# Attention's product with W as seven block products, and an order of work that is planned five times

## The chip, the cores and the metric

The kernel runs on one core of one Trainium2 chip. The metric is device time in microseconds (us) of one execution. The core has these engines: PE (TensorE, matrix products; its weight loads, PEld, run beside them), DVE (VectorE), ACT (ScalarE), POOL (GpSimd) and SP, which here only issues DMAs.

## The reference, cut to what matters

```python
# x: 128 graphs x 128 nodes x 256, float32; adj: 128 x 128 x 128, about 1/8 ones
h = relu(layernorm(x))
for i in range(3):                                   # a gated graph network, OUT = 256
    aggr = einsum('bst,bsd->btd', A, h @ weight[i])
    h = gru_cell(aggr, h, w_ih, w_hh, b_ih, b_hh)
x = x + h
h = relu(layernorm(x))                               # graph attention
Wh = h @ W                                           # W: 256 x 256
s = Wh.sum(-1)
e = where(adj == 0, -inf, leaky_relu(s[:, :, None] + s[:, None, :], 0.2))
x = x + softmax(e) @ Wh
```

The kernel computes the last line as (softmax(e) @ h) @ W: first the weighted sums of h, then their product with W. That product is what changes.

## The kernel before, in words

**Groups and phases.** The 128 graphs are worked on in 32 groups of 4 (G = 4, NG = 32). Each group passes three layers of the graph network and then attention. The 96 pairs (group, layer) are put one after another in `turns` (line 919), so that three groups at different layers are in flight; each pair has a slot of SLOT = 18150 ns.

**A planner orders everything.** Nothing is issued when the Python code meets it. Each piece of work is recorded with `op(engine, ns, function, reads, writes, ...)` (line 75): an engine, an assumed duration, and the buffers it touches. At the end `Plan.run` (line 122) counts due times back through the dependences (`rank_all`), and then places the operations one by one in an imagined course of the five engines, always the one that can begin first, by due time among equals. The order it finds is the order in which each engine gets its instructions; real semaphores hold the dependences. Once built, the order on each engine is fixed.

**The chain.** The products of the graph network (`product`, L719, 128x256 results; `product_rows`, L733, 128x384) form a chain whose order is given beforehand. Each gate product is a block scheme with seven products in place of eight; its data-side sums are made by `node_sums` (L688, L690, L692: on POOL for the state, on DVE for the neighbour sums). `DATA`, `unit` and `source` (lines 696 to 705) say which block or sum each of the seven products takes.

**Between the chain's products** PE gets the side work: `edge_sums` (L645: 12 short bf16 matmuls to a bank, the neighbour sums as exact three-part products), `weighted` (L674: attention's weighted sums, four 128x128 matmuls to each of two banks) and `rows_product` (L1110: the product with W). All of these use two PSUM banks, tag "misc", which the planner gives out as they come free.

**rows_product**, lines 1104 to 1121: for each pair of graphs it takes one misc bank, and for each graph and each half k of the 256 inputs multiplies a 128x128 block of uT (the transposed weighted sums, the stationary operand) by 256 columns of W. DVE then scales each graph's 256 columns by 1/denominator (rden) and adds them to x1 (L1119). A group has 8 such matmuls and 4 such additions. `inner` and late groups do the same in smaller steps.

**The beginning.** `weights()` (line 404) loads and transposes the weights; `compose` (L474) multiplies weight[i] with w_ih once for each layer, and `block_sums` forms the sums of weight blocks, for layer 0 on DVE and for the others and w_hh on POOL. In the first EARLY = 3 groups PE transposes the normed rows (`rows_to_T`, L555); later groups do it with two ACT copies, two DMA transposes and two ACT copies (`turned_halves`, L581, L591, L585).

**In the profile** every fp32 matmul has two records, since PE passes its data twice, and so has its weight load; a transpose of fp32 and a bf16 matmul have one.

Of the kernel before, what the change touches and what calls it, by code (L numbers as in the profile page):

```python
# [13 lines left out]
OP = mybir.AluOpType  # L14
AX = mybir.AxisListType

P = 128
G = 4
# [4 lines left out]
EARLY = 3  # L23
# [3 lines left out]
MARGIN = 7000  # L27
TIMED = 4
KB = 3
# [12 lines left out]
class Plan:  # L42
# [13 lines left out]
    def __init__(self, tags):  # L56
        self.tags = tags
        self.nodes, self.last, self.group, self.due, self.chain = [], {}, 0, 0, []
        self.marks, self.turns, self.waiting, self.phase = {}, [], {}, 0
# [15 lines left out]
    def op(self, eng, ns, fn, reads=(), writes=(), room=(), due=None, mark=None,  # L75
# [5 lines left out]
        i, deps = len(self.nodes), set()  # L81
        for b in room:
            if b.prev is not None:
                deps.update(a[0] for a in b.prev.accesses)
# [37 lines left out]
    def run(self):  # L122
        nodes = self.nodes
        users = [[] for _ in nodes]
        for i, n in enumerate(nodes):
            for j in n[3]:
                users[j].append(i)
        chain = sorted(self.chain, key=lambda i: nodes[i][5], reverse=True)
        bound = set(chain)
        waiting = {t: [b for _, _, b in sorted(w, key=lambda x: x[:2], reverse=True)]  # L130
                   for t, w in self.waiting.items()}

        after = [list(u) for u in users]
        for tag, w in waiting.items():
# [23 lines left out]
        rank_all()  # L158
        missing = [len(n[3]) for n in nodes]
        behind = [(i, self.marks[mark]) for i, mark in self.turns if mark in self.marks]  # L160
        for i, j in behind:
            nodes[i][5] = rank[j] + nodes[i][1]
            users[j].append(i)
            missing[i] += 1
        rank_all()
        for i, _ in behind:
            rank[i] = -float("inf")
        ready = {e: [] for e in self.LAG}
        at = [0.0] * len(nodes)
# [3 lines left out]
        clock, port, thin = dict.fromkeys(self.LAG, 0.0), 0.0, False  # L173
        slots = {t: [0.0] * n for t, (n, kind) in self.tags.items()
                 if kind in ("free", "turn")}
        order, end = [], 0.0
        while len(order) < len(nodes):
            best = None
            for e, pool in ready.items():
# [3 lines left out]
                for i in pool:  # L183
                    if i in bound and i != chain[-1]:
                        continue
                    t = max(clock[e] + (self.FLIP if thin and e == "PE" and not nodes[i][8] else 0), at[i])
                    for b in nodes[i][4]:
                        if b.slot is None:
                            t = max(t, min(slots[b.tag]))
# [13 lines left out]
            n = nodes[i]  # L203
            done = t + self.ns(i, t)
            clock[e] = done - self.OVER[e]
# [5 lines left out]
            for b in n[4]:  # L211
                if b.slot is None:
                    if b.tag in waiting:
                        waiting[b.tag].pop()
# [1011 lines left out]
```

## Time and profile before

| what | value |
|---|---|
| median of 3 runs (lowest, highest) | 2085.99 us (2085.65, 2086.52) |
| the profiled execution's own time | 2085.63 us |
| its span, first to last instruction | 2083.8 us |
| mean granted TensorE clock | 1.000 |
| PE busy, share of the span | 2075.7 us, 100% |
| DVE busy | 1661.7 us, 80% |
| ACT busy | 1599.6 us, 77% |
| POOL busy | 934.4 us, 45% |
| mean DMA rate | 66 GB/s |

The span lies 1.8 us below the execution's own time. A PE record's end is modelled and lies after the point where the next matmul may start, so records overlap: what a matmul takes from PE is read from the start of one to the start of the next, not from its length.

### The profile page before, as it was taken

What the parts mean: (1) busy time and instruction counts of PE and PEld (TensorE: products, weight loads), DVE (VectorE), ACT (ScalarE), POOL (GpSimd) and SP (SyncE); (2) the same over time, 40 slices, a digit from 0 to 9 for tenths busy, and PEclk for the clock granted to TensorE, in tenths of its full rate; (3) what the DMA queues carried; (4) which work ended last, traced back from release to release, by engine and by line L of the source; (5) the groups of instructions that cost most, each with busy time, mean ns of one, the idle gap of its engine ahead of it and who ended that gap; (6) DMA issues with size and microseconds to landing.
All of it is one profiled execution on the core that took longest, in us unless ns stands there. A gap on an engine that the chain in (4) does not pass through costs nothing.

```text
span 2083.8 us, 30778 instructions
## 1 busy us (share of the span) xinstructions
PE 2075.7 (100%) x10630; PEld 1662.7 (80%) x10630; DVE 1661.7 (80%) x3626; ACT 1599.6 (77%) x2977; POOL 934.4 (45%) x881
## 2 busy tenths in 40 slices
PE   9999999999999999999999999999999999999999
PEld 7887887777887778887778877788777788788776
DVE  7678888788788788788788778788778877878778
ACT  6577887877778687868778868778868777877686
POOL 6445554434454445444454344355344544445330
PEclk9999999999999999999999999999999999999999
DMA  3322323322223233232323232233232223223321
GB/s 117 76 61 46 56 49 74 73 56 60 66 72 66 61 72 66 54 83 61 73 56 81 47 86 61 63 70 81 46 81 61 60 56 78 49 54 66 72 77 40
DMA packets 365148, 137.02 MB, mean 66 GB/s; under 512 B 296384, under 2 KB 364736, under 8 KB 364992
## 3 DMA queue, kind: packets, MB, share of 16 engines
q1 hardware_dynamic: 364992, 135.05, 29.6%
q8 instruction: 84, 1.38, 0.3%
q14 instruction: 72, 0.59, 0.1%
HBM read 45.36 MB, written 16.78 MB: 30 GB/s over the span
## 4 chain that ended last, share of the span: by engine, by line
PE 99%; DMA 0%; DVE 0%; SPq 0%; ACT 0%; issue 0%; DVEq 0%; ACTq 0%
PE y_rz L719 16%; PE q_rz L719 11%; PE x_rz L719 11%; PE y_n L719 8%; PE misc L645 6%; PE y_n L733 6%; PE y_rz L733 6%; PE x_n L719 5%; PE q_n L719 5%; PE misc L1110 5%; PE q_n L733 4%; PE x_n L733 4%; PE q_rz L733 4%; PE x_rz L733 4%; PE misc L674 3%; PE misc L474 1%
## 5 line engine op out<-in xcount | busy, mean ns | idle before, releaser
L602 POOL TENSOR_TENSOR r<-rows 128x512 f32<-128x512 f32 x126 | 150.9, 1217 | 318.5 <-ACT rows L585 171.6
L775 DVE TENSOR_TENSOR t_rz<-t_rz,q_rz 128x512 f32<-128x512 f32 x192 | 131.4, 684 | 127.6 <-ACT t_rz L765 99.6
L688 POOL TENSOR_TENSOR hs<-hT 128x512 f32<-128x512 f32 x96 | 129.3, 1347 | 194.7 <-PE y_n L733 82.0
L765 ACT COPY t_rz<-y_rz 128x512 f32<-128x512 f32 x192 | 112.1, 584 | 125.5 <-PE y_rz L719 78.3
L719 PE MATMUL y_rz<-hs,s_hh 128*128 128x256 f32 x768 | 198.9, 382 | 0.0
L719 PE MATMUL y_rz<-gs,s_x 128*128 128x256 f32 x768 | 197.2, 379 | 0.0
L719 PEld LDWEIGHTS y_rz<-hs,s_hh 128*128 128x128 f32 x768 | 144.1, 190 | 22.9 <-ACT t_rz L765 4.7
L719 PEld LDWEIGHTS y_rz<-gs,s_x 128*128 128x128 f32 x768 | 146.2, 190 | 19.5
L775 DVE TENSOR_TENSOR t_n<-t_n,q_n 128x512 f32<-128x512 f32 x192 | 131.0, 682 | 32.5 <-ACT t_n L765 18.9
L605 POOL TENSOR_TENSOR p<-r 128x512 bf16<-128x512 f32 x126 | 153.3, 1234 | 0.2
L692 POOL TENSOR_TENSOR hs<-hT,hs 128x256 f32<-128x256 f32 x96 | 73.1, 761 | 171.2 <-PE q_n L733 118.8
L909 POOL TENSOR_TENSOR x<-x,u 128x512 f32<-128x512 f32 x60 | 80.9, 1364 | 134.4 <-DMA x<-in_x_dram 96.5
L719 PE MATMUL x_rz<-hT,s_hh 128*128 128x256 f32 x512 | 131.4, 379 | 0.0
L719 PE MATMUL x_rz<-aT,s_x 128*128 128x256 f32 x512 | 131.4, 379 | 0.0
L648 ACT COPY aT<-misc 128x512 f32<-128x512 f32 x190 | 105.9, 584 | 22.2 <-PE misc L645 20.4
L622 POOL TENSOR_TENSOR d<-hT,pl 128x512 f32<-128x512 f32 x64 | 80.3, 1256 | 87.1 <-ACT pl L620 40.7
L719 PE MATMUL y_n<-hs,s_hh 128*128 128x256 f32 x384 | 114.4, 380 | 0.0
L719 PE MATMUL y_n<-gs,s_x 128*128 128x256 f32 x384 | 114.3, 380 | 0.0
L1110 PE MATMUL misc<-w,uT 128*128 128x256 f32 x480 | 112.8, 379 | 0.0
L719 PEld LDWEIGHTS x_rz<-hT,s_hh 128*128 128x128 f32 x512 | 97.4, 190 | 19.2
L688 DVE TENSOR_TENSOR gs<-aT 128x512 f32<-128x512 f32 x96 | 78.6, 819 | 37.6 <-ACT aT L648 37.2
L719 PEld LDWEIGHTS x_rz<-aT,s_x 128*128 128x128 f32 x512 | 97.4, 190 | 13.0
(286 smaller groups left out, 6286.7 us busy)
## 6 DMA issues: line engine op xcount, KB each, us to landing
rows<-in_x_dram SPq DMA_DIRECT2D x32, 512.0 KB, 4.1
x<-in_x_dram SPq DMA_DIRECT2D x32, 512.0 KB, 3.9
out_dram<-x SPq DMA_DIRECT2D x31, 512.0 KB, 3.1
at<-in_adj_dram SPq DMA_DIRECT2D x32, 256.0 KB, 2.9
plT<-pl SPq DMA_TRANSPOSE x186, 3.3
peT<-pe SPq DMA_TRANSPOSE x60, 3.1
e<-in_L_gnn_weight_dram SPq DMA_DIRECT2D x3, 256.0 KB, 5.2
rz<-in_L_gnn_w_ih_dram SPq DMA_DIRECT2D x2, 384.0 KB, 4.3
```

The lines of the kernel that those rows point to most:

```text
L602: op("POOL", 1042, lambda part=part: nc.gpsimd.tensor_tensor(ap(r1)[:, part], ap(rows)[:, part], top(rows)[:, part], OP.subtract), [(rows, ...
L605: op("POOL", 1042, lambda part=part: nc.gpsimd.tensor_tensor(ap(p3)[:, part], ap(r1)[:, part], top(r1)[:, part], OP.subtract), [(r1, n, n ...
L622: op("POOL", 1158, lambda k=k, r=r: nc.gpsimd.tensor_tensor(ap(r), ap(hT)[:, k], part(pl, k, 0), OP.subtract), [(hT, 2 * k, 2 * k + 2), (p ...
L645: nc.tensor.matmul(flat(ps)[:, b * N:(b + 1) * N], part(i, b, k), ap(a)[:, b, :], start=(i == 0), stop=(i == 2))
L648: op("ACT", 590, lambda k=k, ps=ps: nc.scalar.copy(ap(dst)[:, k, :], flat(ps)), [ps], [(dst, 2 * k, 2 * k + 2)])
L688: op(eng, cost, lambda: sub(ap(w)[:, 0:2, :], blocks()[:, 1::2, :], blocks()[:, 0:2, :], OP.subtract), [t], [(w, 0, 2)], two=True)
L719: nc.tensor.matmul(ap(bank)[:, half, :], ap(w)[:, i - 1, gate, :], source(i, t, sums), start=(first and c == 0 and m == 0), stop=False, sk ...
L733: op("PE", 645, lambda c=c, w=w, t=t, sums=sums: nc.tensor.matmul(flat(bank)[:, c * P:(c + 3) * P], source(i, t, sums)[:, m * N:(m + 1) * ...
L765: op("ACT", 590, lambda: nc.scalar.copy(ap(t), ap(y)), [y], [t], mark=mark)
L775: op("DVE", 690, lambda: nc.vector.tensor_tensor(ap(t), ap(t), ap(q), OP.add), [q], [t])
L909: op("POOL", 1273, lambda cols=cols, part=part: nc.gpsimd.tensor_tensor(part(x1), part(x1), ap(u)[:, cols], OP.add), [(u, 2 * lo, 2 * hi)] ...
L1110: nc.tensor.matmul(ap(ps)[:, b, :], ap(uT)[:, k, (m + b) * N:(m + b + 1) * N], ap(w1)[:, k, :], start=(k == 0), stop=(k == KD - 1))
```

## The change

1. **Seven block products** (`seven_products`) take the place of `rows_product` in groups 0 to 25 (`g < NG - 6`). For each pair of graphs the transposed sums are seen as 2 x 2 blocks, and so is W. Seven products, each of one block or sum of blocks of uT with one block or sum of blocks of W, take the place of the eight. Each product is two matmuls of 128x128 (one for each graph of a pair). Four sums of blocks of W are made once, on POOL, in the tile w1, which grows to 8 blocks. The data-side sums are made in each group by DVE, into h1, when the weighted sums have been taken from it. The results gather in three half banks X, Q and Y; both misc banks are held. Product 1 goes into X, ACT copies X to Y, and products 2, 7, 6, 5, 3 and 4 add to X, Q and Y, while DVE takes partial results from Y between its products: 12 additions of 128x128 in place of 4 of 128x256.
2. **PSUM's written marks.** Edge sums and whole weighted sums now start a bank once, not each region, so that the whole bank counts as written (`set_bits`); other users of the bank unset the mark. Where the second bank isn't marked when product 1 begins, a matmul with zeros is put in.
3. **The plan.** `run` now places everything PASSES = 5 times (`place`) and keeps the plan whose imagined end is earliest. After each pass `latest` counts new due times back from that plan, with the buffers as it gave them out and with PE's idle time after START taken out; the operations of groups 27 and later (LAST) keep their first due times, moved as a whole. A misc buffer's users get urgent due times as soon as it is given out.
4. **The beginning.** EARLY goes from 3 to 1: groups 1 and 2 are now transposed by DMA. The load of w_hh is recorded with a longer time to landing (5000 in place of 3300 ns).

```diff
-EARLY = 3
+EARLY = 1
+URGENT = 10 ** 9
+PASSES, START, LAST = 5, 20000, 27
...
+        given = list(rank)
+        for _ in range(PASSES):
+            order, end, why, begun, clock, slot = self.place(users, list(rank), bound)
+            if best is None or end < best[0]:
+                best = end, order, clock, slot, begun, why
+            rank = self.latest(users, begun, slot, bound, given)
...
+                    if b.tag == "misc":
+                        for u in b.users:
+                            rank[u] = min(rank[u], t - URGENT)
...
-        "w1": (1, "all", const, [P, KD, D]), "w1_out": (1, "all", const, [P, KD]),
+        "w1": (1, "all", const, [P, 8, P]), "w1_out": (1, "all", const, [P, KD]),
...
-        load(w_hh_nat, nat, w_hh.rearrange("(c p) e -> p c e", p=P), 768)
+        load(w_hh_nat, nat, w_hh.rearrange("(c p) e -> p c e", p=P), 768, lag=5000)
...
+        for i, j, k, f in ((4, 1, 3, OP.add), (5, 4, 0, OP.subtract), (6, 0, 1, OP.subtract), (7, 2, 5, OP.subtract)):
+            op("POOL", 400, lambda i=i, j=j, k=k, f=f: nc.gpsimd.tensor_tensor(
+                ap(W["w1"])[:, i], ap(W["w1"])[:, j], ap(W["w1"])[:, k], f),
+               [(W["w1"], j, j + 1), (W["w1"], k, k + 1)], [(W["w1"], i, i + 1)])
...
-                                         ap(a)[:, b, :], start=(i == 0), stop=(i == 2))
+                                         ap(a)[:, b, :], start=(b == 0 and i == 0), stop=(i == 2),
+                                         skip_group_check=True)
+                set_bits(ps)
...
-        for m in range(lo, hi, 2):
+        if g < NG - 6:
+            seven_products(h1, uT, x1, rden)
+        for m in range(lo, hi, 2) if g >= NG - 6 else ():
...
+    def seven_products(sums, uT, x1, rden):
+        op("DVE", 690, lambda: nc.vector.tensor_tensor(
+            ap(sums)[:, 0:2, :], blocks_of(uT)[:, 1::2, :], blocks_of(uT)[:, 0:2, :], OP.subtract),
+           [uT], [(sums, 0, 2)], two=True)
+        op("DVE", 426, lambda: nc.vector.tensor_tensor(
+            ap(sums)[:, 2, :], ap(sums)[:, 1, :], blocks_of(uT)[:, 0, :], OP.add),
+           [uT, (sums, 1, 2)], [(sums, 2, 3)], two=True)
+        op("DVE", 426, lambda: nc.vector.tensor_tensor(
+            ap(sums)[:, 3, :], blocks_of(uT)[:, 2, :], ap(sums)[:, 2, :], OP.subtract),
+           [uT, (sums, 2, 3)], [(sums, 3, 4)], two=True)
+        one, two = buf("misc"), buf("misc")
+        X, Q, Y = (one, 0), (one, 1), (two, 0)
+        COLUMN = [None, 0, 2, 7, 3, 4, 5, 6]
+
+        def multiply(bank, i, first=False, room=()):
+            (b, h), c = bank, COLUMN[i]
+
+            def mm():
+                if first and written.get(two.slot) is None:
+                    nc.tensor.matmul(flat(two), zeros[:, :P], zeros, start=True, stop=True,
+                                     skip_group_check=True)
+                for m in range(2):
+                    nc.tensor.matmul(ap(b)[:, h, m * P:(m + 1) * P], source(i, uT, sums)[:, m * N:(m + 1) * N],
+                                     ap(W["w1"])[:, c], start=(first and m == 0), stop=True,
+                                     skip_group_check=True)
+                if first:
+                    set_bits(one)
+                    set_bits(two)
+            op("PE", 444, mm, [unit(i, uT, sums), (W["w1"], c, c + 1)], [(b, h, h + 1)], room)
+
+        def add(bank, j, n):
+            b, h = bank
+            for m in range(2):
+                i = 2 * n + m
+                op("DVE", 286, lambda i=i, m=m: nc.vector.scalar_tensor_tensor(
+                    ap(x1)[:, i, j * P:(j + 1) * P], ap(b)[:, h, m * P:(m + 1) * P], ap(rden)[:, i:i + 1],
+                    ap(x1)[:, i, j * P:(j + 1) * P], op0=OP.mult, op1=OP.add),
+                   [(b, h, h + 1), rden], [(x1, i, i + 1)])
+
+        multiply(X, 1, True, [two])
+        op("ACT", 390, lambda: nc.scalar.copy(ap(two)[:, 0], ap(one)[:, 0]), [(one, 0, 1)], [(two, 0, 1)])
+        multiply(X, 2)
+        add(X, 0, 0)
+        multiply(Q, 7)
+        multiply(Y, 6)
+        add(Y, 1, 0)
+        multiply(Y, 5)
+        add(Y, 1, 1)
+        add(Q, 1, 1)
+        multiply(Y, 3)
+        add(Y, 0, 1)
+        multiply(Q, 4)
+        add(Q, 1, 0)
```

## The prediction

> **What bounds the kernel now.** I read the page's busy times first, then the chain that ended last, then PE's own waits, and then the timeline of one stretch in the middle, for what a matmul takes from PE.
>
> ```profile
> PE 2075.7 (100%) x10630; PEld 1662.7 (80%) x10630; DVE 1661.7 (80%) x3626; ACT 1599.6 (77%) x2977; POOL 934.4 (45%) x881
> PE 99%; DMA 0%; DVE 0%; SPq 0%; ACT 0%; issue 0%; DVEq 0%; ACTq 0%
> ```
>
> PE is busy for the whole span, and the chain runs along PE alone: no other engine releases anything late. PE's waits by line:
>
> ```profile
> PE misc L374 <- DMA rz<-in_L_gnn_w_hh_dram: 1.4, 1, 1.4
> PE y_rz L332 <- DVE zeros L329: 1.2, 1, 1.2
> PE x_rz L1171 <- DVE eT L1169: 0.6, 1, 0.6
> PE misc L463 <- DMA e<-in_L_gnn_weight_dram: 0.4, 2, 0.2
> ```
>
> All of these lie in the first 18 us or the last 10. Records overlap, so a pause under 0.17 us could hide; but starts in the middle follow each other evenly. So the time is the sum of what the matmuls take from PE, plus a beginning and an end. What they take is read from start to next start:
>
> ```profile
> 1011.02 0.86 PE L733 MATMUL x_n<-s_hh,hT 128*128 128x384 f32 x2
> 1011.72 0.81 PE L733 MATMUL x_n<-s_x,aT 128*128 128x384 f32 x2
> 1012.36 1.89 PE L1110 MATMUL misc<-w,uT 128*128 128x256 f32 x8
> 1014.09 0.81 PE L733 MATMUL q_rz<-s_hh,hs 128*128 128x384 f32 x2
> ...
> 1015.38 1.95 PE L674 MATMUL misc<-eT,h 128*128 128x128 f32 x16
> 1017.16 0.81 PE L733 MATMUL q_n<-s_hh,hs 128*128 128x384 f32 x2
> ```
>
> Eight records of the product with W take 1014.09 - 1012.36 = 1.73 us, 0.216 each. Sixteen records of 128x128 fp32 take 1.78 us, 0.111 each, with a new stationary block each. A pair of 128x384 records takes 0.645 us, but 0.70 where bf16 edge sums stand before it: 0.055 more at such a step.
>
> **The change part by part.** The built order of the changed kernel has 40 matmuls of `rows_product` left of 248, 364 matmuls of `seven_products`, 8 transposes of `rows_to_T` of 24, and the same 8 matmuls with zeros as before: the filling with zeros is never needed. Steps from bf16 to fp32: 98, before 100.
>
> 1. Removed on PE: 208 matmuls, 416 records x 0.216 = 89.9 us. Added: 364 matmuls, 728 records x 0.111 = 81.0 us (by 1.78/16). **Net -8.9 us.** No cover is involved, since PE is the bound.
> 2. EARLY: 16 transposes less. Four of them take 0.44 us (26.50 to 26.93 in the timeline), so **-1.8 us**. Steps from bf16 to fp32: 2 x 0.055 = -0.1. In return, for each of two groups, ACT gets four copies (two like L581 of 1.04, two like L585 of 1.35 us, where two of 0.59 go) and SP two DMA transposes (3.3 us to landing on the page). These lie beside PE: group 1's rows are normed by 23.6 us in before and its first chain product begins at 42.6, and the built order keeps a whole layer of group 0 between. If that cover were gone, two copies, a landing and a copy back would show, 2 x 1.04 + 3.3 + 1.35 = 6.7 us, once.
> 3. Beginning: PE waits 1.38 us for w_hh. In the new order the load of w_hh stands ahead of the group's rows and adjacency on SP (about 1.1 us sooner by SP's issue times, 2.81 against 3.96), and 0.86 us of `compose` stands ahead of the waiting transpose. Gain between 0 and 1.5, taken as -1.2. Against it, layer 1's block sums now stand on POOL ahead of group 0's state sums: five operations of 1.0 to 1.25 us more before L688's successor, while PE gets 5.2 us of `compose` ahead of that point (two of 1.72, two of 0.86). The two nearly cancel; between 0 and +1.0, taken as +0.5. Behind POOL's late sums the whole chain would wait. **Together -0.7 us.**
> 4. Loops between PE and other engines, new in 26 groups. The built order has the same pattern in nearly all of them: products 1 and 7, one chain matmul of 0.645, products 2 and 6, two chain matmuls, product 5, two chain matmuls, products 3 and 4. A result is usable 0.17 us after its last pass has streamed (1.03 for four records that take 0.86), and DVE begins 0.04 later (x_rz ends at 2080.10, L1174 begins at 2080.14). I take another 0.04 back to PE, an estimate from that row.
>
> ```profile
> L875 DVE SCALAR_TENSOR_TENSOR u<-rz,y_rz 128x128 f32<-128x128 f32 x32 | 9.1, 284 | 3.4 <-ACT rz L871 2.8
> L1119 DVE SCALAR_TENSOR_TENSOR x<-misc,rden,x 128x256 f32<-128x256 f32 x120 | 52.9, 475 | 42.6 <-PE misc L1110 42.2
> L907 DVE TENSOR_TENSOR d<-rows,u 128x512 f32<-128x512 f32 x60 | 59.1, 992 | 16.4 <-ACT u L889 16.4
> ```
>
> An addition of 128x128 from PSUM takes 0.284 us. Product 1 to 2: ACT's copy of 128x256 is 0.36, so 0.17 + 0.04 + 0.36 + 0.04 = 0.61 against 0.444 + 0.645 = 1.09. Product 6 to 5: DVE has X's two additions in front, which push Y's by 0.13; 0.34 + 0.57 + 0.04 = 0.95 against 1.29. Product 5 to 3: 0.82 against 1.29, with one add of the chain (L775's successor, 0.68) in DVE's queue before it, which has 0.35 us to spare. Product 5 to 4: four additions, 1.38 against 1.73. So each loop has 0.3 to 0.5 us in hand, and PE loses nothing while DVE is no later than that. When an addition is late, the following short product waits, and the whole chain queues behind it on PE; DVE's next chain addition stands behind it too. Lower bound 0. Upper bound: DVE lengthens where POOL works beside it (L907 has a mean of 992 ns; L848, the same shape, has 755, so up to 0.3 us late); if all four loops of 26 groups overshot by 0.2, the longest short wait of a weight load on ACT that the waits show, it would be 20.8 us. I take **+1.0 us**, nearest to the stalls of the middle of before, which are next to nothing in spite of many such hand-offs.
> 5. DVE: per group 12 x 0.284 - 4 x 0.475 = +1.5 us, and sums like L688, L690 and L692 on DVE, 0.82 + 0.72 + 0.62 = 2.2 us. 26 x 3.7 = 96 us, 1662 to about 1758, 84% of the span. ACT: 26 x 0.36 = 9 us. POOL: four sums of W once. All stay under PE: cost 0, as long as DVE's queue is not late (4).
> 6. Both misc banks are held for about 7 us in a group (6.3 us from product 1 to the end of product 4, then the last additions). In the built order the next edge sums come about 5.8 us of chain matmuls after product 4: cost 0. A gap without banks would stop aT, and one slot later the chain.
> 7. Planning again: the middle of before has no visible stalls to remove, so 0; at the end, the same products stand after the last chain matmul, 23 us from the end: 0, with +-0.5.
>
> A rule that speaks against step 1: the Trainium skill, "TensorE: Matmul & The Clock Gate", section "Packing small matmuls — row/col tiling", says that a weight load overlaps a running matmul only when it targets other rows of the array, and the section on loading the stationary operand puts a load at columns / 1.2, here 107 ns. The change adds 312 loads; unhidden they would cost 33 us and the sum would be 23 us slower. The row of 16 records in 1.78 us, each with its own full load, does not agree: there is no room for 107 ns beside each pass.
>
> **Sum:** -8.9 - 1.8 - 0.1 - 0.7 + 1.0 = -10.5 us. From the profiled execution's 2085.63 (span 2083.8 and 1.8 around it) that gives 2075.1; its time is 0.36 below the median of the runs, so **2075.4 us**, 0.5% faster.
>
> **The rivals.**
> - *Partial loss (17%).* Late DVE additions or the beginning cost 3 to 6 us: 2077.5 to 2081.8. For: DVE rises to 84%, and three of its kinds are lengthened by POOL. Against: spare time in each loop.
> - *More gained (12%).* The plan also removes the beginning's waits and the short pauses at banks: up to 3 us more, 2072 to 2073.5.
> - *Slower: DVE's place in the loops (6%).* If DVE reaches the additions late by more than the spare 0.35 us in every group, PE stops. The point of balance is 10.5 / 26 = 0.4 us lost per group; with three loops of 0.3 us each the loss is 23 us and the time 2098. For: L907's lengthening. Against: these additions read PSUM, and rows like L875 with a bank show 0.28 to 0.29 without lengthening.
> - *No change (5%).* The shorter matmuls don't keep 0.111 in pairs between 128x384 ones: at 0.122 (8 us more), the gain of step 1 is gone and 2083 is left. For: only runs of eight and sixteen are shown. Against: the runs start and end without a pause.
> - That planning again does nothing, since the first of the five plans is kept, would leave the forecast as it is.
>
> **How the numbers follow.** Forecast 60%, more gained 12%, partial loss 17%, no change 5%, slower 6%. The range 2072.5 to 2081 leaves out slower, no change, and the ends of two others. 0.2% is 4.2 us, about what a measurement of this kernel can tell from no change: faster means under 2081.8: 0.89; within: 0.05; slower: 0.06.
>
> **What would show it.** PE still 100% busy and the chain on PE; records of the new products 0.111 us apart; L674-like pairs between chain matmuls without a pause; DVE near 1750 us; no wait of PE for w_hh. Wrong would be: PE or PEld waiting for DVE's additions or ACT's copy some 0.1 us or more in each group, or edge sums waiting for a bank.

## The result, and the profile after

The changed kernel takes **2097.77 us** (median of 6 runs, 2095.43 to 2099.45), the kernel before 2086.32 beside it (6 runs): a ratio of **1.0054, 95% interval 1.0042 to 1.0067**. It is 11 us slower; the forecast was 2075.4, faster, so its sign was wrong. The execution profiled took 2098.24 us, with a span of 2096.2 and a clock of 1.0.

The page after, busy times and the chain that ended last:

```profile
PE 2074.9 (99%) x10926; PEld 1657.4 (79%) x10926; DVE 1742.7 (83%) x3912; ACT 1618.8 (77%) x3007; POOL 933.9 (45%) x885
PE 90%; ACT 4%; DVE 2%; DMA 2%; issue 1%; SPq 0%; DVEq 0%; ACTq 0%; POOL 0%
```

PE's share falls only from 100% to 99%, since its records overlap, but the chain tells: before, 99% of it ran along PE; now about 10% is ACT, DVE, DMA and issue. Other engines release PE late. The waits of PE's weight loads after (total us, times, longest) say which:

```profile
PEld y_rz L817 <- ACT t_rz L863: 18.2, 34, 1.9
PEld misc L1252 <- ACT misc L1270: 11.2, 24, 0.5
PEld misc L557 <- DVE h L463: 2.1, 1, 2.1
```

L817 is the chain's product (L719 before) and L863 ACT's copy in front of it (L765); before, that wait was 4.7 us in 22 times, the longest 0.2. A weight load that waits is not yet a pause of PE, as loads run ahead. So I also summed PE's **pauses**: from one matmul record's start to the next, less the even pace of the record before, where the difference is over 0.025 us. The even pace is the median in these traces: 0.111 us for 128 columns of fp32, 0.216 for 256, 0.323 for 384, 0.429 for 512, and 0.056 for 128 columns of bf16.

| us | before | after | difference |
|---|---|---|---|
| PE's matmuls, each at its even pace | | | -10.7 |
| pauses in the beginning (first 45 us) | 5.7 | 7.3 | +1.6 |
| pauses in the middle | 7.8 | 25.8 | +18.1 |
| pauses in the end (last 26 us) | 2.2 | 4.7 | +2.5 |
| rest, below that bound | | | +0.9 |
| span | 2083.8 | 2096.2 | +12.4 |

PE's work shrank as forecast, and twice as much is lost in pauses. The middle's are: 14 between a chain y_n and the next y_rz (10.5 us, up to 1.62), 24 inside product 2 (0.10 each, 2.4), 34 inside y_rz products whose weight load is just in time (0.08 or 0.10 each, 3.1; before 22 of 0.08, 1.7), the steps from bf16 to fp32 (5.4, before 5.5), and single ones.

**One of the 14, read backwards.** PE after, at its pause, then ACT in front of it, then SP (start, duration, engine, line; in brackets the idle time before and what ended it):

```profile
1373.13 1.13 PE L817 MATMUL y_rz<-hs,s_hh 128*128 128x256 f32 x4 [1.46 <-ACT t_rz L863]
```

```profile
1366.78 1.35 ACT L1350 COPY s_all<-peT 128x1024 uint16<-128x1024 uint16 x1 [2.89 <-DMA peT<-pe]
1367.99 0.61 ACT L863 COPY y_rz<-x_rz 128x512 f32<-128x512 f32 x1
...
1369.58 2.54 ACT L678 COPY rows<-plT 128x1024 uint16<-128x1024 uint16 x2
...
1372.52 0.57 ACT L863 COPY t_rz<-y_rz 128x512 f32<-128x512 f32 x1
```

```profile
1359.70 0.37 SPq L1057 DMA_DIRECT2D x<-in_x_dram  x1
1360.83 1.24 SPq L1347 DMA_TRANSPOSE peT<-pe  x1
1362.18 4.46 SPq L684 DMA_TRANSPOSE plT<-pl  x2
```

PE waits for ACT's copy of 1372.52. From 1366.78 to 1373.09 ACT has no gap: it stands behind its own wait of 2.89 us for peT, the transposed scores. That transpose was issued at 1360.83 and landed 5.9 us later. The planner counts 3.5 for it (1.283 on SP's queue and a lag of 2.2). A load of x, 512 KB, had been issued 1.1 us ahead. A packet of instructions, 16 KB, also falls into the transpose's time; it begins 2.6 us behind the issue. The DMA queues from 1360 to 1367 us (packets, MB, share of 16 engines):

```profile
q8 instruction: 1, 0.02, 1.4%
```

So a wait of ACT for a DMA that nobody else needs yet is paid by the chain, four copies later. Of the 14 pauses, 11 (8.9 of the 10.5 us) have such a wait for peT in front, and one a wait for plT, the transposed rows. The kernel before, SP in the same stretch:

```profile
1356.94 15.60 SPq L1186 DMA_TRANSPOSE peT<-pe  x2
...
1387.33 0.37 SPq L959 DMA_DIRECT2D x<-in_x_dram  x1
```

There x is loaded where no transpose is near. ACT's waits for that transpose, before and then after:

```profile
ACT s_all L1189 <- DMA peT<-pe: 1.4, 2, 0.7
```

```profile
ACT s_all L1350 <- DMA peT<-pe: 33.1, 21, 2.9
```

In the whole trace, 65 of 250 transposes are issued with a load of x into x1 under way, before 6 of 246. Nor has ACT time to spare: in the median its copy to s_all starts 0.59 us after the landing in before and 0.02 in the changed kernel, where 23 of 30 such copies start within 0.2 us (before: 5 of 30).

### The profile page after: what moved, and what is told of

It is laid out like the page before. It is cut to its first block, busy times and chain, and to the rows that moved or that the text cites. A ratio compares the mean times of both kernels' runs of the same rounds, so it can differ in the third digit from the quotient of the medians.

```text
span 2096.2 us, 31691 instructions
## 1 busy us (share of the span) xinstructions
PE 2074.9 (99%) x10926; PEld 1657.4 (79%) x10926; DVE 1742.7 (83%) x3912; ACT 1618.8 (77%) x3007; POOL 933.9 (45%) x885
## 4 chain that ended last, share of the span: by engine, by line
PE 90%; ACT 4%; DVE 2%; DMA 2%; issue 1%; SPq 0%; DVEq 0%; ACTq 0%; POOL 0%
PE y_rz L817 15%; PE x_rz L817 10%; PE q_rz L817 9%; PE y_n L817 7%; PE misc L738 6%; PE y_rz L831 6%; PE y_n L831 5%; PE x_n L817 5%; PE q_n L817 5%; PE misc L1252 4%; PE x_n L831 4%; PE x_rz L831 4%; PE q_rz L831 4%; PE q_n L831 4%; PE misc L770 3%; ACT rows L678 1%
## 5 line engine op out<-in xcount | busy, mean ns | idle before, releaser
L817 PE MATMUL y_rz<-hs,s_hh 128*128 128x256 f32 x768 | 200.3, 383 | 8.5 <-ACT t_rz L863 8.3
L873 DVE TENSOR_TENSOR t_rz<-t_rz,q_rz 128x512 f32<-128x512 f32 x192 | 131.4, 684 | 88.0 <-ACT t_rz L863 47.6
L817 PE MATMUL y_rz<-gs,s_x 128*128 128x256 f32 x768 | 197.1, 379 | 0.0
L863 ACT COPY t_rz<-y_rz 128x512 f32<-128x512 f32 x192 | 111.9, 583 | 102.5 <-PE y_rz L831 62.4
L790 POOL TENSOR_TENSOR hs<-hT,hs 128x256 f32<-128x256 f32 x96 | 78.6, 819 | 216.8 <-PE q_n L831 198.7
L817 PEld LDWEIGHTS y_rz<-hs,s_hh 128*128 128x128 f32 x768 | 141.0, 190 | 35.2 <-ACT t_rz L863 18.2
L817 PEld LDWEIGHTS y_rz<-gs,s_x 128*128 128x128 f32 x768 | 145.9, 190 | 19.8
L873 DVE TENSOR_TENSOR t_n<-t_n,q_n 128x512 f32<-128x512 f32 x192 | 131.0, 682 | 18.5 <-PE q_n L831 10.4
L1264 DVE SCALAR_TENSOR_TENSOR x<-misc,rden,x 128x128 f32<-128x128 f32 x312 | 87.6, 342 | 58.3 <-PE misc L1252 58.2
L817 PE MATMUL x_rz<-hT,s_hh 128*128 128x256 f32 x512 | 131.5, 379 | 0.4 <-ACT rz L937 0.4
L817 PE MATMUL x_rz<-aT,s_x 128*128 128x256 f32 x512 | 131.4, 379 | 0.0
L715 POOL TENSOR_TENSOR d<-hT,pl 128x512 f32<-128x512 f32 x64 | 75.9, 1202 | 119.7 <-ACT pl L713 119.0
L946 DVE TENSOR_TENSOR d<-hT,u 128x512 f32<-128x512 f32 x128 | 113.6, 888 | 13.4 <-ACT u L943 13.2
L943 ACT ACTIVATE u<-u,bias_i 128x512 f32<-128x512 f32 x128 | 92.1, 723 | 36.0 <-DVE u L934 35.8
L949 DVE SCALAR_TENSOR_TENSOR d<-rz,d 128x512 f32<-128x512 f32 x128 | 113.5, 898 | 1.6
L817 PE MATMUL y_n<-hs,s_hh 128*128 128x256 f32 x384 | 114.3, 379 | 0.0
L817 PE MATMUL y_n<-gs,s_x 128*128 128x256 f32 x384 | 114.2, 379 | 0.0
L817 PEld LDWEIGHTS x_rz<-hT,s_hh 128*128 128x128 f32 x512 | 97.1, 190 | 20.1 <-ACT rz L937 0.8
```

The costliest lines, as they stand in the source:

```text
L817: nc.tensor.matmul(ap(bank)[:, half, :], ap(w)[:, i - 1, gate, :], source(i, t, sums), start=(first and c == 0 and m == 0), stop=False, sk ...
L863: op("ACT", 590, lambda: nc.scalar.copy(ap(t), ap(y)), [y], [t], mark=mark)
L873: op("DVE", 690, lambda: nc.vector.tensor_tensor(ap(t), ap(t), ap(q), OP.add), [q], [t])
L943: op("ACT", 723, lambda j=j, cols=cols: nc.scalar.activation(ap(u)[:, cols], ap(u)[:, cols], AF.Tanh, bias=ap(W["bias_i"])[:, 2 * KD + j:2 ...
L946: op("DVE", 690, lambda j=j, d=d, cols=cols: nc.vector.tensor_tensor(ap(d), ap(hT)[:, j, :], ap(u)[:, cols], OP.subtract), [(hT, lo, hi), ...
L949: op("DVE", 690, lambda d=d, cols=cols: nc.vector.scalar_tensor_tensor(ap(d), ap(rz)[:, 1, cols], 1.0, ap(d), op0=OP.add, op1=OP.mult), [( ...
```

## The experiments

Each expectation names its own theories; in the first four runs, theory 1 is that the x load beside the transposes costs the time, and theory 2 that the seven products or the order do. Behind each time stand, in brackets, its ratio to the before that was measured beside it and the 95% interval; then the pauses of PE in the beginning / middle / end. The before of the first four runs was 2085.82.

**x_after.** After the order is found, the load of x goes behind the same group's two transposes plT on SP.

```diff
+        for last, load_x in moved:          # the second plT transpose, the load of x
+            a, b = order.index(load_x), order.index(last)
+            if a < b:
+                order.insert(b, order.pop(a))
```

> The changed kernel with one thing moved: each group's 512 KB load of x into x1 is issued on SP behind the two transposes of the same group (plT) in place of in front of them. The order on PE, DVE, ACT and POOL is the same instruction by instruction. Theory 1 (the load beside the transposes): in the changed kernel the load stands right in front of peT's transpose in nearly every group, peT lands late (up to 5.9 us), ACT's copy of peT (L1350) waits 33 us in all at the head of ACT's queue, the evictions to t_rz behind it are late, and PE pauses at y_rz (14 pauses, 10.5 us). It expects the wait of that copy under 8 us, those pauses under 2 us, and 2086 to 2090 us. Theory 2 (more work): ACT and DVE are late because seven products give them more to do and hold both misc banks; it expects no change, 2095 to 2099.

2092.7 us (1.0032, 1.0021 to 1.0044), pauses 7.4 / 20.0 / 4.7. The pauses from y_n to y_rz fall from 14 (10.5 us) to 7 (3.65), ACT's wait for peT from 33.1 to 13.0. The direction is theory 1's; none of its sizes was reached.

**x1_small.** From the fourth group on, x is loaded for one graph of four; so three quarters of x are left out of the last sum.

```diff
-                    ap(x1), x[graphs]...
+                    ap(x1)[:, :n], x[g * G:g * G + n]...      # n = 4, from group 3 on 1
```

> The changed kernel with the load of x into x1 cut to a quarter (one graph of four, 128 KB) from group 3 on; the order of every queue is the same. It leaves out three quarters of x in the last sum, so its output differs. Theory 1: if it is the transfer that slows the transposes, a quarter of it takes most of the delay away: median landing of peT back to about 3.2 us, wait of ACT's copy under 10 us, 2086 to 2091 us. If the delay comes from the load's place on SP (issue time, the wait for its buffer) and not from its bytes, peT stays late and the time stays at 2095 to 2099. Theory 2 (more work on ACT and DVE): 2095 to 2099 as well.

2091.34 us (1.0025, 1.0016 to 1.0035), 7.1 / 18.3 / 4.7. The place in the queue is the same as in the changed kernel and only the bytes are fewer: it is the transfer that delays the transpose, not the issue. The 14 transposes peT that are issued with the load under way and have no packet of instructions beside them land in 3.2 us in the median; the 14 such in the changed kernel took 4.2. ACT's wait for peT falls to 11.9 us. In x_after 6.9 us over before remain, here 5.5.

**both.** x_after, and product 7 behind ACT's copy of product 1.

```diff
+        for seventh, copied in sevenths:    # PE's work from product 7 to the copy, product 7 among it,
+            ...                             # is recorded behind ACT's copy
```

> The load moved as in the first run, and besides product 7 of each group recorded behind ACT's copy of X, so that product 1 signals its end by itself; the order on each engine stays as it is. In the changed kernel ACT's copy waits for product 7 (it begins 0.09 us after product 7's end, 0.53 after product 1's), product 2's weight load waits for the copy, and 24 pauses of 0.10 us stand inside product 2, 2.4 us in all. Theory: these go, so 2 to 3 us below the run with the load moved alone (theory 1: 2083.5 to 2088). If the pauses come from something else (weight loads of short matmuls as such), the same time as that run.

2107.78 us (1.0104, 1.0087 to 1.0121), 7.1 / 36.6 / 4.7: the expectation fell. PEld's waits:

```profile
PEld misc L1254 <- ACT misc L1272: 17.9, 25, 1.0
```

Product 2's pauses are gone, but product 7 pauses in their place, 24 times: 0.7 us in front of it in the mean and 0.10 inside it, 19.2 us. The copy reads half of the tile `one`, product 7 writes its other half, and dependences are kept for whole tiles. So whichever of the two is recorded first, the other waits for it. In the changed kernel it is the copy that waits for product 7.

**eight_five.** The changed planner, beginning and marks, with eight products everywhere: `if g < NG - 6` becomes `if g < 0`.

> The changed planner, beginning and marks, but the product with W as eight products in all groups, as before. Theory 1: the order decides by where it puts the load of x and the transposes; here the load stands in front of peT only in some groups, as in before, so 2083 to 2090 us. A rival to it, that planning again with due times counted back leaves ACT's copies without margin whatever the product is: 2093 or more. Theory 2 (the seven products' own work) also expects 2083 to 2088; it is told from theory 1 by the other runs.

2089.08 us (1.0015, 1.0006 to 1.0025), 7.6 / 8.9 / 4.9. Without the seven products the middle is nearly that of before; beginning and end lose as much as in the changed kernel. So these two losses do not need the seven products; but the beginning's stands in other places (the pause of 1.91 us that early3 shows, next, isn't in this run). Only 8 of its transposes are issued with a load of x into x1 under way, so this run doesn't separate the products' work from their order; the runs with other orders, below, do.

The next four ran beside a before of 2085.51.

**early3.** The changed kernel with `EARLY = 3`.

> The changed kernel with the first three groups turned by TensorE again (as in the kernel before), instead of one: 16 transposes come back to PE (+1.8 us by the 0.111 of such a record), and the two groups' DMA transposes and their copies go. The middle's order stays almost the same. Theory 1: the beginning's extra pauses (7.3 us before 45 us against 5.7 before the change) come from the two groups turned by DMA; then the pauses fall by about 1.6 and the time stays near 2097.6 (2096.5 to 2098.7). Theory 2: they come from what stands in front of group 0's work now (the load of w_hh in front, the four sums of W's blocks, group 0's own order); then the pauses stay near 7.3 and the time rises by 1.8, to about 2099.5.

2097.2 us (1.0054, 1.0039 to 1.0069), 7.6 / 23.0 / 4.7. The beginning's pauses stay, as theory 2 has it. The time did not rise by 1.8, since the middle lost 2.8 less, which is not much more than two executions of one order can differ by (u29, below). So this run doesn't show EARLY's saving, which rests on the count of records alone; it shows that EARLY is not what costs the beginning. There the longest pause is one of 1.91 us at 20.9 us, which is in the changed kernel and in early3 and not in before:

```profile
20.91 1.56 PE L557 MATMUL misc<-x,uT 128*128 128x512 f32 x3 [1.75 <-DVE h L463]
```

`compose` (L557) has moved ahead and waits for DVE's copy (L463) of a transposed weight. Which of the planner's changes moved it was not separated.

**u29.** The priority of a begun misc bank only below group 29.

```diff
-                    if b.tag == "misc":
+                    if b.tag == "misc" and self.group_of[i] < 29:
```

> The changed kernel, but the planner's rule that whatever uses a begun misc bank comes before everything else holds only for groups below 29. The order differs from the changed kernel's in the last stretch alone (17 lines of PE's order), where it is the order of the kernel before, save for one product one place later. Theory 1: the end's extra pauses (4.7 us in the last 26 us against 2.2) come from that rule, which draws all of the last groups' products with W forward and leaves none to stand in PE's waits; then they fall to 2.2 to 2.6, the time by 2 to 2.5 us, to about 2095.3. Theory 2: they come from something else (the replanned middle delivers late to the end): the pauses and the time stay, 2097.7 within 0.8.

2094.55 us (1.0044, 1.0029 to 1.0059), 7.5 / 23.6 / 2.2. The end's loss is gone, as theory 1 has it. The end after, and the end in u29:

```profile
2077.09 2.05 PE L1212 MATMUL q_rz<-w,uT 128*128 128x256 f32 x8 [0.72 <-ACT uT L777]
2082.41 0.92 PE L1312 MATMUL y_n<-w,uT 128*128 128x256 f32 x3 [0.46 <-ACT uT L1306]
```

```profile
2071.70 2.75 PE L1212 MATMUL misc<-w,uT 128*128 128x256 f32 x12
2074.30 1.89 PE L1212 MATMUL q_rz<-w,uT 128*128 128x256 f32 x8
```

In u29, as before, products of an earlier group stand ahead of the q_rz product while ACT makes its uT. The priority draws all of them forward, and PE waits. PE's order is otherwise that of the changed kernel, and yet the middle shows 23.6 in place of 25.8: so middles of single executions that differ by some 2 us can't be told apart.

**p7_third.** x_after, with product 7 behind product 2 on PE.

```diff
+        for seventh, second in sevenths:
+            a, b = order.index(seventh), order.index(second)
+            if a < b:
+                order.insert(b, order.pop(a))
```

> The kernel with the x load behind the two transposes, and in addition product 7 behind product 2 on PE, in all groups where the plan had it in front; nothing else changes its place. Theory 1: the copy of product 1 waited for product 7 only because both lie in one tile; now the copy can start 0.44 us sooner, product 2 finds it ready, product 7 stands behind the copy's reader anyway, and the 24 pauses inside product 2 (0.10 each in the records, 2.4 us) go: 2092.7 - 2.4 = 2090.3 (2089.5 to 2091). Additions of X start 0.44 later, since their tile is then product 7's too, for which the loop to product 5 has room. Theory 2: the pauses are the price of any copy between the two products: no change, 2092.7. Theory 3: the later additions hold up product 5 or the chain's additions: slower than 2094.

2093.62 us (1.0038, 1.0023 to 1.0053), 6.9 / 21.4 / 4.7: product 2's 24 pauses stay (2.44 us). PE and ACT in the changed kernel, then both in p7_third:

```profile
1349.22 0.61 PE L1252 MATMUL misc<-w,h 128*128 128x128 f32 x4
1349.67 0.81 PE L831 MATMUL y_rz<-s_hh,hs 128*128 128x384 f32 x2
1350.33 0.71 PE L1252 MATMUL misc<-w,uT 128*128 128x128 f32 x4
```

```profile
1349.92 0.36 ACT L1270 COPY misc<-misc 128x256 f32<-128x256 f32 x1 [0.65 <-PE misc L1252]
```

```profile
1343.21 0.61 PE L1254 MATMUL misc<-w,uT 128*128 128x128 f32 x4
1343.65 0.81 PE L831 MATMUL y_rz<-s_hh,hs 128*128 128x384 f32 x2
1344.32 0.71 PE L1254 MATMUL misc<-w,uT 128*128 128x128 f32 x4
```

```profile
1343.91 0.36 ACT L1272 COPY misc<-misc 128x256 f32<-128x256 f32 x1 [0.20 <-PE misc L1254]
```

The copy does start behind product 1 now (1343.82 by its record's end), but the room is the same. From the end of the record in front: 0.09 to the copy, 0.36 for it, 0.05 to product 2's start, which is when one chain product ends; and its second pass then comes 0.10 late, 0.71 for four records instead of 0.61. One chain product between is 0.1 us too little, so theory 2 holds here.

**sp19_u29.** The planner, not the computation, corrected: SP's time for a transpose 1.9 us instead of 1.283 (to landing 3.48 as before), x loaded when the turned rows are copied back, and u29's line.

```diff
-        op("SP", 1283, lambda: nc.sync.dma_start_transpose(   ... lag=2200)
+        op("SP", 1900, lambda: nc.sync.dma_start_transpose(   ... lag=1583)
-                    ap(x1), x[graphs].rearrange("b n d -> n b d")), [], [x1])
+                    ap(x1), x[graphs].rearrange("b n d -> n b d")), [rows], [x1])
```

> The changed kernel with three corrections of the planner and none of the computation: it counts 1.9 us of SP's queue for each DMA transpose instead of 1.283 (the total to landing the same), it loads x only when the group's turned rows have been copied back, and the rule for begun misc banks holds below group 29 only. Theory 1 (the loss is transposes that land later than the plan counts, plus the end): the stream keeps its -10.7, the middle's pauses fall from 25.8 to between 10 and 14 (7.8 as before, 2.4 inside product 2, and a few), the end to about 2.4, the beginning stays at about 7.3: 2085.8 - 10.7 + 1.6 + 0.2 + 2 to 6 = 2079 to 2083, faster than the kernel before. Theory 2 (the loops of the seven products themselves take what they save): 2088 or more, with the pauses in the lines of the seven products and the chain's additions.

2096.42 us (1.005, 1.0033 to 1.0067), 6.9 / 27.3 / 2.2: neither theory's time with its reason. The end is right and ACT no longer waits for peT, but 23 pauses of some 0.5 us stand between y_n and y_rz, one in nearly every group. In front of one of them, DVE and POOL:

```profile
1300.53 1.80 DVE L1005 TENSOR_TENSOR d<-rows,u 128x512 f32<-128x512 f32 x1
1302.25 1.35 DVE L973 SCALAR_TENSOR_TENSOR u<-rz,t_rz 128x128 f32<-128x128 f32 x1
1303.52 0.68 DVE L873 TENSOR_TENSOR t_n<-t_n,q_n 128x512 f32<-128x512 f32 x1
```

```profile
1300.50 1.27 POOL L1007 TENSOR_TENSOR x<-x,u 128x512 f32<-128x512 f32 x1 [16.62 <-ACT u L987]
1301.73 1.72 POOL L786 TENSOR_TENSOR hs<-hT 128x512 f32<-128x512 f32 x1
```

Two of DVE's operations take 1.80 and 1.35 us beside POOL's sums, where the fastest tenth of such operations in this trace stays under 0.69 and 0.28. The chain's addition (L873) comes 2.2 us late, ACT stands 2.25 us for it and is then full until the pause. In 20 of the 23 pauses this wait stands in front, in 2 a wait for peT. So in this order DVE is the late one; that POOL is what lengthens it is read from the trace, and no run tested it. The Trainium skill, "SBUF — State Buffer", section "Who interferes with whom", says that DVE and GpSimd share one port pair that one of them holds for a whole instruction; a lengthening of about one POOL operation agrees with that.

The next four ran beside a before of 2086.37.

**once.** `PASSES = 1`.

> The changed kernel with the first of its five plans alone. In its order the seven products stand one chain product wider (two chain products between 1 and 2, where the fifth plan has one), so both misc banks are held 0.65 us longer; the load of x stands behind the group's transpose of the scores instead of ahead of it, though still ahead of the two transposes of the rows. Theory 1 (what is lost in the middle is transposes that land late behind the x load): ACT's waits on the scores' transpose shrink below 33 us and the 24 pauses of product 2 go, so the time is lower than 2097.7, at 2090 to 2095. Theory 2 (planning again is what lets the products' banks come free in time, as it was meant to): PE waits for banks in many groups, the time is over 2100.

**2149.93 us** (1.031, 1.0284 to 1.0336), 6.7 / 73.4 / 4.9. Theory 1 missed the time, though product 2 has no pauses and ACT's wait for peT falls to 3.6 us, as it expected. Theory 2's "over 2100" came true, but not for its reason: no bank is waited for. PEld's waits in once, and ACT:

```profile
PEld y_n L817 <- ACT t_n L869: 46.7, 22, 3.2
```

```profile
1011.43 1.34 ACT L678 COPY rows<-plT 128x1024 uint16<-128x1024 uint16 x1 [2.00 <-DMA plT<-pl]
```

Here the x load stands between peT and plT, and plT lands late. ACT waits 2 us and is then full past the chain's next copy. There are 21 such pauses in front of y_n, 41.5 us. But only 6 of them (9.2 us) have a wait for plT right in front; in 7 (17.6 us) it is a wait for DVE's L1171, and in the others for DVE or for PE itself. So late transposes are a part of this loss, and where the greater part comes from stays open. With seven products the further plans are worth 52 us, and the one that is kept still loses.

**plt_half.** x_after, where the two transposes of rows (third layer, from group 3 on) turn one of two planes; the other half of those rows' bits is left out.

> The kernel with the x load behind the two transposes; in addition those two transposes (the rows of the third layer, from the fourth group on) turn only one of their two planes, and the other plane of the turned tile keeps what an earlier group left there: half of the bits of these rows are left out. The order of every engine is unchanged. Theory 1 (what is left of the pauses between the chain's y_n and y_rz products comes from three transposes in a row, which land late together, so that ACT stands in front of their copies): ACT's wait on the scores' transpose (13.0 us) falls by more than half, the pauses (7, 3.65 us) fall below 1 us, the time to 2089 to 2090.5. Theory 2 (they come from ACT's and VectorE's queues being full there, VectorE lengthened by GpSimd): the waits on the transpose may fall, but the pauses and the time stay, 2092.7 within 0.8.

2091.4 us (1.0026, 1.0016 to 1.0037), 7.5 / 19.1 / 4.7. The pauses from y_n to y_rz stay (6, 3.83 us), and ACT's wait for peT too (12.9). So three transposes in a row are not what makes peT late. Theory 1 fell here, without theory 2 being shown.

**sp17** and **sp21.** As sp19_u29, with 1.7 or 2.1 us on SP's queue and 3.9 to landing. In sp21's order product 7 of the last group with seven products stands ahead of product 1, so one half of that group's output columns is another sum; the work is the same.

> The changed kernel with the planner corrected in three places: a DMA transpose counts 1.7 us on SP's queue and 3.9 to landing (1.283 and 3.48 before), x is loaded only when the turned rows have been copied back, and the rule for begun misc banks ends below group 29. Theory 1 (a plan whose transposes take what the trace shows loses nothing by them): pauses in the middle of 10 to 14 us, in the end 2.2, and 2080 to 2084. Theory 2 (any replanned order packs ACT and VectorE so tightly that another late hand-off takes the place of the one removed, as in the run with 1.9 and 3.48): 2090 to 2097, with the pauses again between the chain's y_n and y_rz products.

> As the run with 1.7 and 3.9, with 2.1 us of SP's queue for a transpose and 3.9 to landing. Theory 1: 2080 to 2085. Theory 2: 2090 to 2097; and, being another order from the same rules, it differs from the run with 1.7 by several us in either direction, which would show how much of the time is the luck of one order.

sp17: 2084.77 us (0.9994, 0.9984 to 1.0003), 8.0 / 13.7 / 2.6, within 1 us of theory 1's range and not clearly faster than before. sp21: 2088.32 us (1.0009, 1.0000 to 1.0018), 6.9 / 17.2 / 2.6. Another order from the same rules differs by 3.5 us.

**x_shift.** Open was what makes peT late in x_after, in every third group. The instruction queue has a packet of 16 KB some 24 us apart. x_after, with 29 matmuls of four columns ahead of PE's first, so that these packets move against the work:

```diff
+    for _ in range(29):
+        nc.tensor.matmul(phys["y_rz", 0, 0]...[:, :4], zeros[:, :P], zeros[:, :4], start=True, stop=True, ...)
```

> The kernel with the x load behind the two transposes, and 29 matmuls of four columns with zeros ahead of PE's first one (58 instructions more at the start of PE's stream; their banks are filled with zeros anew right behind). Nothing else changes place. Theory 1 (a packet of instructions beside a transpose makes it late): 16 KB hold some 24 us of PE's instructions, so 58 more move every later packet some 5.5 us earlier against the work; by the packets' times in the trace none then falls into the first 4 us of a scores' transpose in the middle. The pauses between y_n and y_rz (3.65 us) fall below 1.5, ACT's waits on the scores' transpose (13.0 us) by half; the extra matmuls cost 1 to 3 us at the beginning, so the time is 2091 to 2094. Theory 2 (full queues): the pauses stay at 3 to 4 us in the same groups (984, 1175, 1367, 1559 us), and the time is 2093 to 2096.

2091.14 us (1.0025, 1.0015 to 1.0035), 6.4 / 18.7 / 4.7, beside a before of 2086.13. Against PE's matmuls the packets moved by 5.4 us in the median, as expected, but not evenly: most by 3.0 to 7.8. DMA queues (packets, MB, share of 16 engines) and landings (median us) of x_after from 1356 to 1361 us:

```profile
q8 instruction: 1, 0.02, 1.1%
...
peT<-pe SPq DMA_TRANSPOSE x1, 5.1
```

In x_shift this transpose has no packet beside it and lands in 3.2 us. The next group's, from 1419 to 1424 us in x_shift:

```profile
q8 instruction: 1, 0.02, 1.7%
...
peT<-pe SPq DMA_TRANSPOSE x1, 4.8
```

In x_after that one has no packet beside it and lands in 3.2 us. Lateness goes where the packet goes. The pauses at 348, 985, 1176, 1368 and 1559 us are gone; new ones stand at 411, 603, 1239 and 1431. In sum the pauses are 2.96 us, not below 1.5, and ACT's wait for peT is 9.9 us, not half of 13.0, since the packets now meet others. All five pauses of x_after that begin with a wait for peT (2.5 us) have a packet that begins 0.9 to 3.3 us behind the transpose's issue, and so have the four new ones (1.8 us), which have none in x_after. So theory 1's mechanism is shown, and its size was not reached. The two pauses left in both runs, near 180 and 1816 us, begin with waits for DVE and for PE.

**sp16b, sp175, sp21b.** sp17's rules with product 7 tied behind product 1, and 1.6 / 1.75 / 2.1 us on SP's queue, 3.9 / 3.9 / 3.8 to landing.

> The corrected rules (x load behind the turned rows, the rule for begun banks below group 29 only, product 7 tied to come behind product 1) with 1.6 us of SP's queue and 3.9 us to landing for a transpose. Theory 1 (the seven products keep their 10.7 us, and what is lost is a matter of where late transposes, additions and copies meet the chain): pauses in the middle of 9 to 16 us and a time of 2080 to 2086, near the run with 1.7 and 3.9 (2084.8). Theory 2 (the seven products leave too little room whatever the order): 2088 or more.

> As the run with 1.6, with 1.75 us of SP's queue and 3.9 to landing. Theory 1: 2080 to 2086. Theory 2: 2088 or more.

> As the run with 1.6, with 2.1 us of SP's queue and 3.8 to landing. Theory 1: 2080 to 2087 (the earlier plan with 2.1 and 3.9 gave 2088.3, with 1.3 us in one place). Theory 2: 2088 or more.

2085.85 us (0.9999, 0.9990 to 1.0009); 2083.88 (0.9989, 0.9980 to 0.9998); **2083.70** (0.9988, 0.9979 to 0.9997; 10 runs), 6.9 / 14.4 / 2.2 for the last. All are within theory 1. The last two beat both kernels, by 2.2 and 2.4 us the one before and by about 14 the changed one, with the same work and only its order changed. They are the best of six orders from such corrected rules. ACT's wait for peT in sp21b:

```profile
ACT s_all L1352 <- DMA peT<-pe: 3.0, 4, 1.0
```

## Why the prediction was wrong, step by step

| step | forecast | measured |
|---|---|---|
| 1, 2 stream of PE (products, transposes, steps) | -10.8 | -10.7 |
| 3 beginning | -0.7 | +1.6 |
| 4 loops of the seven products | +1.0 | +3.6 |
| 6 banks | 0 | no pause found |
| 5, 7 other pauses of the middle | 0 | +14.5 |
| 7 end | 0 | +2.5 |
| rest, below the bound of a pause | | +0.9 |

- **Steps 1 and 2 were right.** Records of the new products stand 0.11 us apart, also in fours between chain products. The "no change" rival and the rule on weight loads, whose 33 us would have made the kernel 23 us slower than before, are both excluded.
- **Step 3 had the wrong sign.** PE's wait for w_hh is gone, as forecast. What is late next was named wrongly: not POOL's sums, but DVE's copies of transposed weights, for which PE pauses 0.83 and 1.91 us. It isn't EARLY (early3).
- **Step 4 was mis-sized at one term**: "0.61 against 1.09" for product 1 to 2. With the copy bound to product 7 by the tile, the room is one chain product, and the copy with its hand-offs takes 0.1 more than that (p7_third): 2.4 us. The other 1.2 are single pauses in front of products. The sign of being wrong that the prediction named, some 0.1 us for ACT's copy in each group, came true, but it is a small part of the loss. The DVE loops, which the "slower" rival was built on, held: that rival named the wrong place, and that its 2098 is the measured time is luck.
- **Step 5 held for the busy times** (DVE 1742.7 us, forecast 1758). Its "cost 0 as long as DVE's queue is not late" holds in the changed kernel more or less; sp19_u29 is the order in which it doesn't.
- **Step 7 failed, and with it the sign.** "The middle of before has no visible stalls to remove, so 0" looked at what planning again could remove, not at what a new order could add: 14.5 us in the middle and 2.5 in the end. Before's middle did hold 22 loads of y_rz that wait for ACT's copy, up to 0.2 us each and 1.7 us of PE's pauses, a sign of how little room ACT had. I read the new order of PE for its products and left SP's aside, where the x load stood ahead of peT in nearly every group: 4.6 us by moving it (x_after) and 5.9 by making it smaller (x1_small), each against its own before. Six of the 11 pauses that begin at peT, the three longest among them, had the load and a packet of instructions together (6.9 us); with the load moved, the five that are left behind a late peT, each with a packet, take 2.5 us. No rival had a transfer that lands later than the planner counts. For the end, I compared the products and not the priority that empties it: 2.5 us (u29). The remark that keeping the first of the five plans "would leave the forecast as it is" was far off as well: that plan takes 2149.93 us (once).
- Of the middle's 18.1 us, 5.8 go with the load's place alone (x_after), 11.4 with a better order (sp21b). In sp21b ACT's copy to s_all starts 0.95 us after the landing in the median, in the changed kernel 0.02. Its middle still has 6.6 more than before, 2.5 of it product 2's. What the rest of it consists of stays open.

## What to carry to other kernels

When a scheduler replans, read the new order of the DMA queue as closely as that of the engine that bounds the kernel, and compare what the planner counts for a transfer with its landing in the trace when other transfers run. Where the bound engine is full, as here, a saving shows only as far as the in-order engines around it have slack; look for the waits of an engine for something that isn't urgent, because what is queued behind them is. The same work in two orders of one set of rules differed by several us here, so a change that moves an order needs several orders measured before it is judged.

## What the runs showed of the hardware

- **A DMA transpose is late beside a 512 KB load.** In the changed kernel the transposes peT with neither a load or store of 256 KB or more nor a packet of instructions beside them land in 3.0 to 3.3 us (24, median 3.1). With the load of x into x1 under way and no packet they land in 3.9 to 5.3 (14, median 4.2), with both in 3.7 to 5.9 (9, median 5.0). With a quarter of the load's bytes (x1_small) and no packet it is 3.2 to 3.7 (14, median 3.2).
- **It can be late beside a packet of instructions.** In the changed kernel 86 packets of 16 KB come some 24 us apart and take 0.9 to 2.0 us (median 1.1). Of the transposes peT with a packet that begins 1.9 to 3.3 us behind the issue, 7 of 8 land in 4.4 to 5.2 us in x_after and all 6 in 4.4 to 4.9 in x_shift; but in before 5 of 8 land in 3.0 to 3.1. So such a packet alone doesn't decide it, and what does stays open. The Trainium skill, "DMA: Bandwidth & Descriptors", section "Queues, rings and completion order", says that each DMA engine takes turns between queues by whole packets; the late rows agree, though they are late by somewhat more than one packet's time.
- **A weight load that is released just in time costs about 0.1 us** inside its product: 0.10 in product 2 (24 times), 0.08 or 0.10 in y_rz (17 times each; before 22 times 0.08).
